# Four engines of a graph-network kernel take their instructions in source order from layer 1 on

## The chip, the cores and the metric

The kernel runs on one core of one Trainium2 chip. The metric is the device time in microseconds (us) of a whole execution. Five engines matter: PE (TensorE, matrix products; its weight loads are counted apart as PEld), DVE (VectorE), ACT (ScalarE), POOL (GpSimd) and SP (SyncE, which here only issues DMA transfers). Each engine works through its own list of instructions, and an instruction may wait for a semaphore that another engine or a transfer raises.

## The reference

A graph of 3125 nodes and 103125 directed edges (50000 random ones, the same turned round, and a self loop for each node), 128 features per node. Four residual layers follow one another, each inside a layer norm:

```
x = layernorm(x + relu(segment_sum(edge_weight * (x @ W)[src], dst) + b))      # layer 0
x = layernorm(x + gat(x))                                                      # layer 1
x = layernorm(x + attention(x))                                                # layer 2
x = layernorm(x + sigmoid(sage(relu(sage(x)))))                                # layer 3
```

`gat` has 4 heads of 32 features: `e = leaky_relu(a_src[src] + a_dst[dst], 0.2)`, a softmax of `e` over the edges that end in a node, the weighted sum of `(x @ W)[src]`, a bias, a linear skip path and an inner layer norm with gain and bias. `attention` has one head: the softmax over a node's incoming edges of query times key, then the weighted sum of values. A `sage` layer is the mean of the neighbours' features through one matrix plus the node's own through another.

## The kernel before

Nodes are padded to 25 blocks of 128 (`NB`), and every layer is made dense. A first stage turns the edge list into two matrices, through one-hot products on PE: `ctd`, the number of edges between any two nodes (bf16, 25 × 128 × 3200), and `wd`, the sum of their weights, both kept in DRAM. This stage and most of layer 0 share a loop: PE adds `wd` blocks times `x @ W` into five PSUM banks `acc0` (20 blocks of destination nodes; line 794). It ends at line 902 with `front.close()`.

**Layer 1.** What is left of layer 0 (destination blocks 20 to 24, banks `left`, weights loaded as `cw`) is added in a loop over 25 source blocks, and between its steps stand the first tasks of layer 1, by the number of the step (`marks`): `scores1` (transposes of x and the products with the attention vectors; line 1093 copies a part out to `ad`, which goes through the DRAM buffer `add_`), `heads`, `factors` (four exponentials), and from step 13 on four calls of `values(b)`, two blocks each. `values` (lines 1130 to 1144) scales x @ W by two exponentials on DVE and splits the result into three bf16 parts with `split3` (lines 549 to 555): ACT copies, DVE subtracts, ACT copies, DVE subtracts, ACT copies.

Then come 200 items: 4 groups of destination blocks (4, 7, 7, 7 blocks; `IG`), two head pairs each, 25 source blocks each. An item has masks and products. `masks` makes for each of two heads the edge mask for that side of the leaky relu: either an activation `fm` on ACT (line 1225) and a minimum `cm` on DVE (line 1226), or one DVE instruction (line 1219). `products` are three matmuls for each destination block (lines 1236 and 1241). The source writes `masks` two items ahead of `products`; there are 8 `cm` buffers, 5 `fm` and 6 `ct` (the counts from DRAM). In group 0's first head pair nine more calls of `values` stand in every second item. After the last item of a head pair `sums` reduces PSUM into `nz` on DVE (line 1260) and finishes on POOL (lines 1266 to 1269); `quotients` follows, and after the second head pair `finish1`: norm1 (statistics on DVE, a square root on ACT), norm2 (identities on ACT), three POOL operations, a second norm, and the transposes `turns` for layer 2 (line 984 and the lines near it). `skips` (lines 1249 and 1250) adds the skip path. These tasks are spread over items by a list of due steps:

```
def later(k, f):
    due.append((now[0] + k, f))
```

`step()`, called once per item, writes out the tasks that are due, so the source already has them at certain items.

**Layer 2** has 50 items: scores on PE (line 1373), exponential on ACT (1376), product with the counts on DVE (1377), one item ahead of the products with the values (1381). The tasks of `finish1` for the last group of layer 1 stretch into its first items, and `degrees` (line 1356) stands in its fourth. **Layer 3** multiplies with the counts twice (`add1`, line 1476; `add2`, line 1549) with the hidden layer between (`hidden`, lines 1505 to 1507, `around` and `own`, line 1513, which share one PSUM bank `tr`). The end (lines 1565 to 1577) takes seven groups of up to 4 blocks, one after the other in the source: a scaled sum on DVE, a sigmoid on ACT, the residual sum, a layer norm (statistics on DVE, square root on ACT line 767, up to four identities on ACT line 773) and the store.

**What sets the order.** Every engine's list is put in order when the kernel is built, by a scheduler that sees all instructions with their dependences and weaves tasks that don't depend on each other. Once built, the order is fixed. The square root, the exponential and the sigmoid use different function tables on ACT; the compiler puts a table load ahead of an activation whose table isn't in place.

Of the kernel before, what the change touches and what calls it, by code (L numbers as in the profile page):

```python
# [505 lines left out]
def fast_path(  # L506
# [403 lines left out]
        copy(xT[:, b0 * P : (b0 + n) * P], t[:, : n * P])  # L910


    lp = ctx.enter_context(tc.tile_pool(name="f_p12", bufs=1))
    xT = lp.tile([P, NP], F32, name="f_xT")

# [664 lines left out]
@with_exitstack  # L1580
def gnn_kernel(ctx, tc, *args):

    nc = tc.nc
    fl = ctx.enter_context(tc.tile_pool(name="fl", bufs=1))
    flag = fl.tile([1, 1], I32, name="flag")
    fast_path(tc, flag, *args)
    ok = nc.values_load(flag[0:1, 0:1], min_val=0, max_val=1, skip_runtime_bounds_check_because="a comparison's result")
    with tc.If(ok == 0):
        general_path(tc, *args)
# [30 lines left out]
```

## Time and profile before

| | us |
|---|---|
| median of 3 runs | 1537.32 (1535.15 to 1537.59) |
| profiled execution | 1536.56 |
| its span, first to last instruction | 1534.5 |
| PE busy | 1400.5 (91%) |
| DVE busy | 981.0 (64%) |
| ACT busy | 923.4 (60%) |
| POOL busy | 122.5 (8%) |

The span is 2.1 us shorter than the execution's time, which has the start and the end around it. The mean granted TensorE clock was 0.979. In a list of waits or groups, `fm<-adr,bas` is an output and what it is made from, by the program's names, and "<-DVE cm" names what ended a wait. In a timeline each row has its start, its length, the engine, the line, and how many instructions were put together in the row. All line numbers in the text are those of the kernel before; in the changed kernel they are larger by 4 from line 913 on.

### The profile page before, as it was taken

Reading aid. Unit: us, or ns where it says so; the run is one execution under the profiler, and the core shown is the slowest. Engines: PE = TensorE matmul, PEld = TensorE weight load, DVE = VectorE, ACT = ScalarE, POOL = GpSimd, SP = SyncE. Lnnn points to the kernel's source line nnn. Section 1 sums busy time; section 2 is a strip of 40 time slices with the busy share of each in tenths; the row PEclk is TensorE's granted clock in tenths of the full one; section 3 lists DMA queues with packets and bytes.
Section 4 is the critical chain, followed back from the end, with each engine's and each line's share of the span. In section 5 each row is a group of like instructions: output and inputs, shape, how many; then the busy total and the mean of one; then the engine's idle time right before and its main releaser. Section 6 shows DMA issues by size and latency. Waiting matters only on the chain.

```text
span 1534.5 us, 35155 instructions
## 1 busy us (share of the span) xinstructions
PE 1400.5 (91%) x14871; PEld 1223.6 (80%) x14871; DVE 981.0 (64%) x1574; ACT 923.4 (60%) x1880; POOL 122.5 (8%) x136
## 2 busy tenths in 40 slices
PE   4899999999997978899989989899999989999995
PEld 3898999998997867899979889577777764458995
DVE  4999899989991389778878887544464360012005
ACT  2988778888882489878778676544474340023006
POOL 1000000000000023203311320300000000000000
PEclk9999999999999999999999999999999999999998
DMA  6387787878877623444434333332222226513551
GB/s 192 91 220 207 203 234 206 235 202 223 214 214 232 222 85 101 143 118 125 132 115 134 114 87 95 106 94 68 67 72 73 82 105 238 193 44 129 195 195 45
DMA packets 210368, 224.39 MB, mean 146 GB/s; under 512 B 72892, under 2 KB 184007, under 8 KB 209945
## 3 DMA queue, kind: packets, MB, share of 16 engines
q1 hardware_dynamic: 206344, 217.74, 48.4%
q10 hardware_dynamic: 3457, 2.35, 0.6%
q8 instruction: 118, 1.93, 0.5%
q0 software_dynamic: 400, 1.97, 0.4%
q14 instruction: 49, 0.40, 0.1%
HBM read 157.67 MB, written 64.36 MB: 145 GB/s over the span
## 4 chain that ended last, share of the span: by engine, by line
PE 40%; DVE 5%; ACT 2%; issue 1%; POOL 1%; DMA 1%; DVEq 0%; ACTq 0%; SPq 0%; POOLq 0%
PE acc L1381 9%; PE s L1373 8%; PE acc L1476 7%; PE acc L1549 6%; PE acc L1241 4%; PE acc L1236 2%; DVE cm L1226 1%; DVE nz L1260 1%; PE tr L1513 1%; PE acc L1513 1%; DMA ct<-f_ctd 1%; ACT fm L1225 1%; DVE cm L1219 0%; PE tr L1505 0%; PE acc L1505 0%
## 5 line engine op out<-in xcount | busy, mean ns | idle before, releaser
L1241 PE MATMUL acc<-vp,cm 128*128 128x198 bf16 x2500 | 344.7, 252 | 6.6 <-DVE cm L1226 4.1
L1225 ACT ACTIVATE fm<-adr,bas 128x896 bf16<-128x896 f32 (+1 forms) x320 | 286.5, 952 | 68.0 <-DVE cm L1226 63.1
L1236 PE MATMUL acc<-vp,ct 128*128 128x204 bf16 x1250 | 315.2, 256 | 10.0 <-DVE vp L1144 5.6
L1241 PEld LDWEIGHTS <-cm 128*128 128x128 bf16 x2500 | 236.0, 98 | 26.5 <-issue 10.6
L872 PE MATMUL wp<-wod,ohc 128*128 128x128 bf16 x3840 | 244.0, 219 | 8.8 <-ACT cs L877 6.6
L872 PEld LDWEIGHTS <-ohc 128*128 128x128 bf16 x3840 | 224.0, 98 | 9.8 <-issue 9.4
L833 DVE TENSOR_TENSOR wod<-ohd,w 128x4096 bf16<-128x4096 bf16 (+1 forms) x120 | 225.0, 1931 | 0.6 <-PE wp L872 0.6
L1226 DVE TENSOR_TENSOR cm<-fm,ct 128x896 bf16<-128x896 bf16 (+1 forms) x320 | 198.1, 649 | 36.1 <-PE acc L1241 14.1
L842 ACT ACTIVATE wod<-ohd,wu 128x128 bf16<-128x128 bf16 x640 | 197.0, 400 | 0.0
L1377 DVE TENSOR_TENSOR e<-e,ct 128x416 f32<-128x416 f32 (+1 forms) x175 | 110.4, 636 | 108.2 <-ACT e L1376 102.6
L1376 ACT ACTIVATE e<-s,f_nm 128x416 f32<-128x416 f32 (+1 forms) x175 | 111.5, 642 | 99.4 <-PE s L1373 94.1
L1381 PEld LDWEIGHTS acc<-self__8127,e 128*128 128x128 f32 x1250 | 148.4, 193 | 21.5 <-issue 19.7
L1373 PE MATMUL s<-yT,f_xT 128*128 128x416 f32 (+1 forms) x350 | 145.8, 552 | 4.6 <-ACT rt L1356 4.0
L1381 PE MATMUL acc<-self__8127,e 128*128 128x129 f32 x1250 | 148.7, 276 | 0.6 <-DVE e L1377 0.6
L794 PE MATMUL acc<-f_xw,cw 128*128 128x128 f32 x1000 | 118.4, 278 | 7.4 <-DMA cw<-wd 7.4
L1236 PEld LDWEIGHTS <-ct 128*128 128x128 bf16 x1250 | 122.4, 98 | 2.5 <-issue 1.5
L883 ACT COPY ws<-wp 128x512 f32<-128x512 f32 x160 | 93.6, 585 | 49.8 <-PE wp L872 48.2
L794 PEld LDWEIGHTS acc<-f_xw,cw 128*128 128x128 f32 x1000 | 115.0, 194 | 7.6 <-DMA cw<-wd 7.6
L864 PE MATMUL cp<-ohc,ohd 128*128 128x125 bf16 x1280 | 96.7, 218 | 21.1 <-ACT ws L883 17.9
L1373 PEld LDWEIGHTS s<-yT,f_xT 128*128 128x128 f32 x350 | 62.2, 191 | 57.7 <-issue 40.6
L1476 PE MATMUL acc<-ct,ip 128*128 128x512 bf16 (+1 forms) x525 | 104.9, 360 | 1.4 <-DMA ct<-f_ctd 1.4
L1549 PE MATMUL acc<-ip,ct 128*128 128x128 bf16 x1875 | 105.2, 219 | 0.0
(277 smaller groups left out, 1482.7 us busy)
## 6 DMA issues: line engine op xcount, KB each, us to landing
ct<-f_ctd SPq DMA_DIRECT2D x50, 800.0 KB
wd<-ws SPq DMA_DIRECT2D x40, 896.0 KB
ct<-f_ctd SPq DMA_DIRECT2D x150, 224.0 KB
cw<-wd SPq DMA_DIRECT2D x50, 640.0 KB
f_ctd<-cs SPq DMA_DIRECT2D x20, 1000.0 KB
ct<-f_ctd SPq DMA_DIRECT2D x25, 416.0 KB
ct<-f_ctd SPq DMA_DIRECT2D x25, 384.0 KB
cw<-wd SPq DMA_DIRECT2D x25, 320.0 KB
```

The lines of the kernel that those rows point to most:

```text
L794: nc.tensor.matmul(accs[j // 4][:, j % 4, :], cw[:, j - h, :], xw[:, i, :], start=False, stop=(i == NB - 1 and (j % 4 == 3 or j == n - 1)) ...
L833: nc.vector.tensor_tensor(f[:, 0:n].rearrange("p w (a t) -> p w a t", t=2), ohd[:, 0:n].rearrange("p w (a t) -> p w a t", t=2), twos(w2[s] ...
L842: nc.scalar.activation(wod[2][:, BW + w, :], ohd[:, BW + w, :], AF.Copy, scale=w3[:, 1, at : at + 1])
L872: nc.tensor.matmul(wp[:, j, :], ohc[:, w, :], wod[s][:, w, :], start=(j == 0 and q == 0 and s == 0), stop=(j == 3 and q == 1 and s == 2), ...
L1225: nc.scalar.activation(f[:, : n * P], at, AF.Relu, bias=bas[:, c, h : h + 1], scale=UP)
L1226: nc.vector.tensor_tensor(m[:, : n * P], f[:, : n * P], ct[:, : n * P], OP.min)
L1236: nc.tensor.matmul(out_(F1, PW), ct[:, k * P : (k + 1) * P], vp[:, c, hp : hp + 2, :, 2 * F1 : V1], start=(c == 0), stop=False, skip_group ...
L1241: nc.tensor.matmul(out_(0, 2 * F1)[:, j], ms[j][:, k * P : (k + 1) * P], vp[:, c, hp + j, :, 0 : 2 * F1], start=False, stop=(c == NB - 1 a ...
L1373: nc.tensor.matmul(s[:, :m], xT[:, c * P : (c + 1) * P], yT[:, i0 * P + a : i0 * P + a + m], start=True, stop=True)
L1381: nc.tensor.matmul(acc[k // 3][:, (k % 3) * (P + 1) : (k % 3 + 1) * (P + 1)], es[q, c][:, k * P : (k + 1) * P], vo[:, c, 0 : P + 1], start ...
L1476: nc.tensor.matmul(acc[k][:, :n], ips[b // 4][:, b % 4, s, :], ct[:, c : c + n], start=(b == 0 and s == 0), stop=(b == NB - 1 and s == 2),)
L1549: nc.tensor.matmul(acc[g][:, j, :], ct[:, (b0 + j) * P : (b0 + j + 1) * P], ups[b // 4][:, b % 4, s, :], start=(b == 0 and s == 0 and j == ...
```

## The change

Between the end of layer 0's shared loop (and the small function `turned`) and the buffers of layer 1, a context is entered that stays open to the end of the kernel. Inside it the instructions of PE, DVE, ACT and POOL are issued in the order in which the source writes them. SP, which issues the transfers, is not in the list and is still placed by the scheduler. No instruction of the source is added, removed or altered; ACT's table loads are placed anew by the compiler, for the new order.

```diff
@@ -910,6 +910,10 @@
         copy(xT[:, b0 * P : (b0 + n) * P], t[:, : n * P])
 
 
+
+    ctx.enter_context(
+        tc.manual_schedule(engines={mybir.EngineType.PE, mybir.EngineType.DVE, mybir.EngineType.Activation, mybir.EngineType.Pool})
+    )
     lp = ctx.enter_context(tc.tile_pool(name="f_p12", bufs=1))
     xT = lp.tile([P, NP], F32, name="f_xT")
 
```

## The prediction

> **What bounds the kernel now.** I read the page's span, busy shares and 40 slices first, then the chain that ended last, the groups with what they waited for, and then one stretch at a time: busy time by window, TensorE's waits by window, and the timeline where an order had to be seen. The page first (a slice is 38.4 us):
>
> ```profile
> PE 1400.5 (91%) x14871; PEld 1223.6 (80%) x14871; DVE 981.0 (64%) x1574; ACT 923.4 (60%) x1880; POOL 122.5 (8%) x136
> PE   4899999999997978899989989899999989999995
> DVE  4999899989991389778878887544464360012005
> ACT  2988778888882489878778676544474340023006
> PE 40%; DVE 5%; ACT 2%; issue 1%; POOL 1%; DMA 1%; DVEq 0%; ACTq 0%; SPq 0%; POOLq 0%
> ```
>
> TensorE is the bound nearly everywhere: it is idle only 1534.5 − 1400.5 = 134 us, so an order can win at most that. It can lose more. The change touches nothing before about 437 us (layer 0's shared loop), so I look after that. Layer 1 runs from about 547 to 958 us, layer 2 to about 1250, layer 3 to the end. Busy time by window (window, length, then PE, PEld, DVE, ACT, POOL, granted clock, DMA share, GB/s):
>
> ```profile
> 547.70:598.80 51.10, 39.60 (x351) 33.73 (x352) 47.78 (x141) 48.44 (x90) 13.44 (x25) 0.93 0.29 86
> 629.20:958.00 328.80, 301.52 (x3215) 290.54 (x3215) 269.27 (x491) 248.51 (x324) 75.46 (x54) 0.98 0.40 117
> 958.00:1000.00 42.00, 36.18 (x196) 25.58 (x194) 21.43 (x69) 24.87 (x46) 12.39 (x10) 0.96 0.34 113
> 1000.00:1250.00 250.00, 250.00 (x1438) 184.55 (x1437) 115.35 (x235) 120.67 (x205) 1.68 (x1) 1.00 0.23 71
> 1505.00:1534.50 29.50, 11.07 (x199) 10.90 (x196) 16.02 (x83) 20.53 (x43) 0.00 (x0) 0.77 0.20 58
> ```
>
> Three kinds of stretch. In the first head pair of group 0 (547.7 to 598.8) DVE and ACT are the bound, 47.8 and 48.4 busy of 51.1: no slack. In groups 1 to 3 and layer 2, PE is, with slack on the others. In the last 29.5 us there is no PE bound but a chain through ACT and DVE.
>
> **What the Trainium skill says.** "PSUM — Partial Sum Buffer", section "Engine vs sequencer instructions": the queues of ScalarE, VectorE and GpSimdE are strict FIFO and matmuls start and complete in program order. So a compiled order is what runs, and an instruction that waits holds all behind it. The trace agrees: no instruction of DVE or ACT overtakes there. "ScalarE: Activation LUTs", section "What ACT_TABLE_LOAD costs": about 1283 ns for the load and about 1380 ns for a drain at each switch. The trace shows the 1.28 us, but no drain after other work: a sigmoid starts at 1507.22 and takes 0.61, the load begins at 1507.86, and the square root starts at 1509.15. I take 1.28.
>
> **The change part by part.** Nothing is added or removed; instructions of PE, DVE, ACT and POOL go in source order instead of an order that the scheduler wove, and the compiler then places ACT's table loads anew. In SP's queue a few stores and loads of `add_`/`adr` shift by a few places; it waits for nothing new that the before order does not already have (its 6 `ct` buffers run ahead).
>
> *A, the rest of layer 0 (437 to 547.7): 0.* The `left` accumulation is fed by `cw` loads at 231 GB/s (437 to 500) and ends with them. The four `values` chains placed among it are hidden under that; from −3 (nothing woven in) to +3 (a chain of 5 us outlasts it).
>
> *B, group 0, heads 0 and 1: +30.* One `values` (L1130–1144) is a ping-pong: DVE scales, ACT copies (L549), DVE subtracts, ACT, DVE, ACT, DVE negates (L1144):
>
> ```profile
> 536.15 0.75 DVE L1134 TENSOR_TENSOR v<-trw,fa 128x256 f32<-128x256 f32 x2
> 536.99 0.63 ACT L549 CAST vp<-v 128x528 bf16<-128x528 f32 x1
> 537.65 0.71 DVE L551 TENSOR_TENSOR vs<-v,vp 128x528 f32<-128x528 f32 x1
> 538.39 0.63 ACT L552 CAST vp<-vs 128x528 bf16<-128x528 f32 x1 [0.77 <-DVE vs L551]
> 539.06 0.71 DVE L554 TENSOR_TENSOR vs<-vs,vp 128x528 f32<-128x528 f32 x1 [0.70 <-ACT vp L552]
> 539.80 0.63 ACT L555 CAST vp<-vs 128x528 bf16<-128x528 f32 x1 [0.78 <-DVE vs L554]
> 540.47 0.64 DVE L1144 TENSOR_SCALAR vp<-vp 128x396 bf16<-128x396 bf16 x2 [0.37 <-ACT vp L555]
> ```
>
> It takes 541.11 − 536.15 = 4.96 us, with DVE working 2.81 and waiting 2.15. At 560 to 600 the scheduler fills these gaps with masks (DVE 38.9 busy of 40). In source order no mask stands between the links on either queue; 9 chains lie here, one every second item: 9 × 2.15 = 19.4. The two `scores1` blocks put an `ad` copy (L1093), which waits for PE, ahead of the masks' activations: about 3 + 2. `factors` has four exponentials with a table load each way: 1.4 not covered. The start: the masks of the first items stand behind the ends of both `left` blocks and the fourth chain, which end near 554, where the before order began masks at 547: +4. Sum 29.8. Bounds: 20 (chains alone) and 40. The later items of PE are behind it, so nothing covers it. The second head pair (598.8 to 629.2) is cover neither way: −1 to +2, I take 0.
>
> *C, groups 1 to 3: +3.* PE works 301.5 of 328.8, so up to 27 us are to be gained. Its longest waits there:
>
> ```profile
> PE few L1249 <- DVE f_xw L1250: 9.7, 5, 3.4
> PE few L984 <- ACT f_x L975: 5.8, 2, 2.9
> ```
>
> These are `skips` and `turns`, which the source spaces one or two items apart (1.85 us each), 9.7 and 5.8 and 4.0 more behind L990, so about 20 us of them should go. Against that, in source order a norm is a block: norm1 is 2.2 us on DVE, the square root needs a table load of 1.28, norm2's seven identities hold ACT 2.8 us ahead of the next mask. Masks are two items ahead, 3.7 us, so about 8 us reach PE where these meet, twice or less in a group, and 3 after each last item for `nz`: I take 30 against 27. Bounds: −15 (the distances of `later` cover nearly all) and +15.
>
> *D, start of layer 2 (958 to 1000): +2.* PE is idle 5.8 now, 4.0 of it at the degrees' transpose. `finish1` of group 3 stretches over layer 2's first items: POOL's three operations of 2.1 us, two norms, table changes between square root and exponential. About 8 against 6. Bounds −3 and +8.
>
> *E, layer 2 (1000 to 1250): 0.* PE is at 250.0 of 250, the others below half. The order can hardly touch it; to +2.
>
> *F, layer 3 up to 1498: +3.* Eight transposes that were moved up go back among the `add1` matmuls (8 × 0.1 = 0.8, an estimate from half a weight load of 0.19, since no row shows them apart), less 0.3 for a quicker drain at 1250; around 1392 to 1412 `own` and `around` share one `tr` bank and wait for a split chain each: 2.5. From 0 to +5.
>
> *G, the end: +13.* Each of seven groups goes sigmoid, add, statistics, square root, identities. Before, two groups share table loads; sigmoids after a load start at 1505.15, 1513.34 and 1521.15, so 7.8 for two groups:
>
> ```profile
> 1519.86 1.28 ACT L1568 ACT_TABLE_LOAD   x1
> 1521.15 0.63 ACT L1568 ACTIVATE t<-t 128x512 f32<-128x512 f32 x1
> 1521.69 1.63 ACT L773 ACTIVATE f_x<-f_xw,ms,sd 128x128 f32<-128x128 f32 x4
> 1523.23 0.29 ACT L1568 ACTIVATE t<-t 128x128 f32<-128x128 f32 x1
> ...
> 1524.02 1.28 ACT L767 ACT_TABLE_LOAD   x1 [0.50 <-DVE sd L766]
> ```
>
> In source order ACT has load, sigmoid, load, square root, four identities for each group, 14 loads in place of 8. The first sigmoid to the last identity of a group: 2.85 to the square root (1521.15 to about 1524.0; its load lies under DVE's 2 us), 0.65 to the first identity (1517.45 to 1518.10), 1.64 identities, then 1.28 for the sigmoid's load: 6.4 to 6.6 with hand-overs. From 1499.7: six periods of 6.5 end at 1538.7, the last group of one block takes 2.5: 1541.2, against 1528.0: +13.2. PE's 3.3 us per group hide under it. From +11 to +15.
>
> Sum: 0 + 30 + 0 + 3 + 2 + 0 + 3 + 13 = 51 on the profiled execution (1534.5 span, 1536.6 with what lies around it, 0.8 below the median of 1537.3). So 1536.6 + 51 = 1588; on the median 1588 too.
>
> **The rivals.**
> *Source order wins in C and D (0.22).* Speaks for it: the source already places `later` steps at distances, masks two items ahead, and PE's waits of 20 us have an owner. C −15, D −3, and B nearer 22: 22 − 15 − 3 + 2 + 13 = +19, 1556; up to about 1565.
> *It is faster (0.06).* The place is group 0: if the DVE gaps in the chains are covered (ACT far enough ahead that DVE loses only the start, 5) and C and D give all but a little of their 33 us, −28: 5 − 28 + 13 + 1 = −9, 1528. It decides where C and D's gain exceeds B plus 13. Against: in B the chains' links follow one another on both queues, which leaves at least 19, so C and D would have to yield everything.
> *Lockstep (0.10).* If ACT's identities and DVE's statistics stall PE at every norm (two norms and a boundary in each of three groups, 8 us each, say 48 above my C) the time is 1588 + 35 or so, 1620; a lower granted clock (0.77 where PE is idle at the end, 0.93 in B) would add to it.
> *Nothing changes (0.02).* Were the two orders alike it would be within 0.2%, about 3 us, which is what a measurement of this kernel can tell. Against: from the first `left` matmuls on, the compiled orders of PE, DVE, ACT and POOL differ everywhere.
>
> **How the numbers follow.** The forecast has 0.60, and 1570 to 1605 as its own range. With the second rival down to 1552 and a part of the lockstep case up to 1613, eight in ten are held. Faster by over 0.2% 0.06, within 0.2% 0.02, slower by over 0.2% 0.92.
>
> **What would show it.** B: chains without a mask between, DVE and ACT at 75 to 85% between 555 and 630, the first `nz` (L1260) near 629 instead of 598.8. C: skips' and turns' waits gone from PE, waits on `cm` L1226 in their place, PE's busy time unchanged. D: PE idle about 8. G: 14 table loads, sigmoids 6.5 apart. I would be wrong if group 0 ends before 615, or if groups 1 to 3 take over 345 or under 314 us against 328.8.

## The result and the profile after

The changed kernel takes 1623.34 us (median of 4 runs, 1623.30 to 1624.44) against 1536.99 for the kernel before in the same comparison: a ratio of 1.0566, 95% interval 1.0547 to 1.0584. It is 86 us slower; 51 were forecast, and the time lies above the stated range (1570 to 1605, with 1613 as the upper end of its wider one).

The page of the changed kernel, span, busy times, slices and chain (a slice is now 40.5 us):

```profile
span 1621.2 us, 35041 instructions
PE 1418.7 (88%) x14858; PEld 1233.6 (76%) x14871; DVE 1006.6 (62%) x1574; ACT 933.6 (58%) x1886; POOL 115.1 (7%) x136
PE   4999999899987766889979889989999989999990
DVE  4999998999933456878879878544455350021013
ACT  3988878887852456878678668444555330032025
PE 41%; DVE 11%; ACT 9%; issue 2%; DMA 0%; ACTq 0%; DVEq 0%
```

The work is the same. What grew is for the most part idle time: PE is idle 202.5 us instead of 134.0, and busy 18 us longer over the same matmuls. In the chain that ended last the share of DVE and ACT grew (5% and 2% before, 11% and 9% now). The hole in all three rows in slices 14 to 16 is the end of the `left` stretch and the first head pair of layer 1's group 0; there TensorE's granted clock fell too (0.76, against 0.93 before). Busy time by window, the stretches that answer to those of before:

```profile
500.00:554.30 54.30, 46.39 (x338) 40.30 (x339) 19.31 (x77) 19.87 (x44) 3.73 (x13) 0.94 0.53 172
554.30:645.00 90.70, 54.54 (x358) 44.37 (x357) 54.75 (x143) 52.53 (x92) 9.06 (x30) 0.76 0.17 48
677.00:1019.00 342.00, 305.37 (x3215) 290.21 (x3215) 280.90 (x492) 247.49 (x324) 73.65 (x54) 0.98 0.39 112
1019.00:1065.00 46.00, 37.66 (x204) 26.32 (x202) 28.38 (x69) 24.33 (x41) 12.78 (x10) 0.94 0.35 111
1065.00:1315.00 250.00, 249.87 (x1435) 184.68 (x1435) 114.11 (x232) 121.79 (x208) 1.68 (x1) 1.00 0.24 69
1570.00:1621.00 51.00, 14.29 (x256) 14.11 (x253) 19.41 (x95) 30.67 (x50) 0.00 (x0) 0.68 0.12 34
```

In 554 to 645 (547.7 to 598.8 before) DVE and ACT, the bound of that stretch, are busy 54.8 and 52.5 of 90.7, 60% and 58%, where they had been full. Landmarks of the two traces put the 86.7 us of the span in place:

| landmark | before | after | later by | added in the part |
|---|---|---|---|---|
| last `left` matmul starts (A) | 545.3 | 554.3 | 9.0 | 9.0 (forecast 0) |
| first `nz` of group 0, first head pair (B) | 598.8 | 645.1 | 46.4 | 37.4 (30) |
| `nz` of group 0, second head pair | 629.2 | 677.0 | 47.8 | 1.4 (0) |
| last `nz` block of group 3 begins (C) | 958.05 | 1019.05 | 61.0 | 13.2 (3) |
| last scores of layer 2 (D, E) | 1249.2 | 1313.7 | 64.5 | 3.5 (2) |
| last `add2` matmuls (F) | 1515.9 | 1584.1 | 68.2 | 3.7 (3) |
| end of the span (G) | 1534.5 | 1621.2 | 86.7 | 18.5 (13) |

### The profile page after: what moved, and what is told of

Read it like the earlier page. It is cut to its first block, busy times and chain, and to the rows that moved or that the text cites. A ratio compares the mean times of both kernels' runs of the same rounds, so it can differ in the third digit from the quotient of the medians.

```text
span 1621.2 us, 35041 instructions
## 1 busy us (share of the span) xinstructions
PE 1418.7 (88%) x14858; PEld 1233.6 (76%) x14871; DVE 1006.6 (62%) x1574; ACT 933.6 (58%) x1886; POOL 115.1 (7%) x136
## 4 chain that ended last, share of the span: by engine, by line
PE 41%; DVE 11%; ACT 9%; issue 2%; DMA 0%; ACTq 0%; DVEq 0%
PE s L1377 7%; PE acc L1385 7%; PE acc L1245 7%; PE acc L1480 6%; PE acc L1553 5%; PE acc L1240 4%; ACT fm L1229 3%; DVE cm L1230 3%; DVE nz L1264 1%; DVE cm L1223 1%; DVE e L1381 1%; ACT f_x L979 1%; DVE bs L965 1%; PE acc L1517 1%; ACT f_xw L979 1%
## 5 line engine op out<-in xcount | busy, mean ns | idle before, releaser
L1245 PE MATMUL acc<-vp,cm 128*128 128x198 bf16 x2500 | 360.5, 257 | 44.1 <-DVE cm L1230 29.5
L1240 PE MATMUL acc<-vp,ct 128*128 128x204 bf16 x1250 | 325.5, 260 | 8.7 <-DVE nz L1264 5.3
L1229 ACT ACTIVATE fm<-adr,bas 128x896 bf16<-128x896 f32 (+1 forms) x320 | 282.6, 950 | 31.7 <-DVE cm L1230 31.4
L1245 PEld LDWEIGHTS <-cm 128*128 128x128 bf16 x2500 | 241.7, 100 | 69.1 <-DVE cm L1230 37.0
L1230 DVE TENSOR_TENSOR cm<-fm,ct 128x896 bf16<-128x896 bf16 (+1 forms) x320 | 207.0, 674 | 58.6 <-ACT fm L1229 49.9
L1381 DVE TENSOR_TENSOR e<-e,ct 128x416 f32<-128x416 f32 (+1 forms) x175 | 114.5, 665 | 119.1 <-ACT e L1380 113.1
L1385 PEld LDWEIGHTS acc<-self__8129,e 128*128 128x128 f32 x1250 | 148.4, 193 | 19.7 <-issue 18.6
```

Of the source, the lines that this page charges most:

```text
L1229: nc.scalar.activation(f[:, : n * P], at, AF.Relu, bias=bas[:, c, h : h + 1], scale=UP)
L1230: nc.vector.tensor_tensor(m[:, : n * P], f[:, : n * P], ct[:, : n * P], OP.min)
L1240: nc.tensor.matmul(out_(F1, PW), ct[:, k * P : (k + 1) * P], vp[:, c, hp : hp + 2, :, 2 * F1 : V1], start=(c == 0), stop=False, skip_group ...
L1245: nc.tensor.matmul(out_(0, 2 * F1)[:, j], ms[j][:, k * P : (k + 1) * P], vp[:, c, hp + j, :, 0 : 2 * F1], start=False, stop=(c == NB - 1 a ...
L1385: nc.tensor.matmul(acc[k // 3][:, (k % 3) * (P + 1) : (k % 3 + 1) * (P + 1)], es[q, c][:, k * P : (k + 1) * P], vo[:, c, 0 : P + 1], start ...
```

## The experiments

All times are medians; what a run gained is against the changed kernel's 1623.3. Most runs have two executions, and the kernel before had medians from 1534.9 to 1537.8 in the comparisons, so a difference of 1 or 2 us says little by itself. In code, lines without a sign show the place, `...` marks a cut, `{...}` stands for the engines, and comments are added here. A line with an L is one of the run whose view is shown.

**Where the loss sits.** `e1_from_layer2`, the context entered only after layer 1:

```diff
-    ctx.enter_context(tc.manual_schedule(engines={...}))   # ahead of layer 1's buffers
+    ctx.enter_context(tc.manual_schedule(engines={...}))
     p3 = ctx.enter_context(tc.tile_pool(name="f_p3", bufs=1))
```

> Source order from layer 2 on only; layer 1 is woven by the scheduler as before. The trace of the changed kernel puts about 4 us of the loss at the start of layer 2, 6 at the middle of layer 3 and 19 at the end: 1537 + 29 = 1566. By the prediction's terms (D 2, F 3, G 13) it would be 1555. If the losses of layer 1 were only passed on to later stages by a lower clock or by late transfers, it is below 1550.

Measured: 1564.1 (ratio 1.0183, 1.0151 to 1.0214), 29 above the kernel before in the same comparison (1534.9), 27 above its 1537.0. The three parts of the table for layers 2 and 3 have 25.7 together, and 26.9 in this run's trace: these layers lose by themselves about what the changed kernel's trace shows for them, so hardly anything is passed on from layer 1.

`e2_from_items`, the context entered ahead of layer 1's items, so that the `left` stretch is woven:

```diff
+        ctx.enter_context(tc.manual_schedule(engines={...}))
         items = [(g, hp, c) for g in range(len(IG)) for hp in range(0, H, 2) for c in range(NB)]
```

> Source order from the items of layer 1 on; the rest of layer 0, with the scores and the first four calls of values, is woven as before. If the order of PE in the left stretch is what makes group 0 start 10 us late, 1623 - 10 = 1613, and the last left matmul starts near 545. If the stretch is bound by its loads, as the prediction has it, and the late start comes from the items' own order, 1620 to 1623.

Measured: 1609.5, 14 less. The last `left` matmul starts at 545.6 and the first `nz` at 630.0, 31.2 later than before. So B, alone, costs what was forecast for it (30), and the order in the `left` stretch costs 15: 9 in the stretch and 6 in the start of the items. The starts of the chains (their first subtraction, L551) show where: from the last `left` matmul to the fifth chain it takes 13.5 us before, 17.3 in this run and 23.9 in the changed kernel; from there to the last chain 35.5, 59.3 and 59.2; from that to `nz` 4.5, 7.8 and 7.8. The 6 us lie ahead of the fifth chain.

`e3_not_the_end`, the context (here called `source`) closed ahead of the last stretch:

```diff
         last = {b: counts(b) for b in range(NB - HB, NB)}
+        source.close()
         for g, (b0, n) in enumerate(GB):
```

> Source order up to the last stretch; the seven groups of the end are woven as before. By the trace of the changed kernel the end costs 19: 1604. By the prediction's term 13: 1610.

Measured: 1604.7, 18.6 less: the end costs what the trace shows.

**The left stretch.** TensorE's waits from 500 to 560 us in the changed kernel (engine and line, what it waited for, total, times, longest):

```profile
PE tr_sa L1091 <- ACT f_xT L532: 3.6, 3, 2.2
PE left L794 <- DMA cw<-wd: 3.1, 1, 3.1
PE acc L1240 <- DMA ct<-f_ctd: 2.2, 1, 2.2
PE tr_sa L1091 <- DVE f_xT L534: 1.6, 2, 0.8
```

`scores1` has a transpose, a copy on another engine, and products that need the copy. In source order PE stands through each copy, and through the first load, with `left` matmuls behind; the scheduler had put these in between. `e7_scores_two_steps` writes the products one or two steps of the loop after the transposes:

```diff
-        marks = {3: lambda: scores1(0), 4: lambda: (scores1(1), scores1(2)), 5: lambda: scores1(3), 6: lambda: scores1(4)}
+        marks = {
+            2: lambda: turn1(0), 3: lambda: (turn1(1), score1(0)), 4: lambda: (turn1(2), score1(1)),
+            5: lambda: score1(2), 6: lambda: turn1(3), 7: lambda: score1(3), 8: lambda: turn1(4), 9: lambda: score1(4),
+        }
...
-        marks[7] = top
-        marks[9] = ...
+        marks[10] = top
+        marks[11] = ...
```

> The changed kernel, with each scores1 of the left stretch written in two steps: transposes and copy at one step of the loop, the products that need the copy at a later one. Theory: the left stretch ends 9 us late because PE, busy 46 of 48 us there before, waits in order for each copy and for the first load; about 5 of it are waits for copies: 1618, last left matmul near 550. Rival: the loads bind the stretch, as the prediction has it: 1623.

Measured: 1621.8, 1.6 less, which by itself is hardly more than the comparisons differ. The stretch itself, first to last `left` matmul, took 47.9 us instead of 51.5 (41.4 before), so this edit gave back 3.6 of the 10; a wait of 1.8 for a copy and the 3.1 for the load are still there. The first `nz` came 3.8 earlier (641.4), but by the last `nz` of group 3 only 1.7 were left. The theory holds in part for the stretch, and half of the gain is used up in later waits.

`e8_pe_woven` takes PE out of the list:

```diff
-        tc.manual_schedule(engines={mybir.EngineType.PE, mybir.EngineType.DVE, ...})
+        tc.manual_schedule(engines={mybir.EngineType.DVE, ...})
```

> The changed kernel without PE in the list: DVE, ACT and POOL in source order, PE woven. If the losses come from the order of DVE and ACT (chains, norms, table loads), only the left stretch's 9 us come back: 1614. If PE's order is the cause of the late start as a whole (15 us in the run whose source order began with the items), 1608. If weaving PE alone hurts, because the scheduler's guess of DVE and ACT is off, over 1623.

Measured: 1609.3, 14 less. The last `left` matmul starts at 545.2, as before: the 9 us of A are PE's order. The first `nz` comes at 639.5, only 5.7 earlier, so B's own chains stay, and of the 9 us 3.4 are used up there. The time is near the 1608 of the second theory, but not for its reason: the late start did not come back as a whole, and the rest of the 14 lies in groups 1 to 3 (3.6) and in layers 2 and 3. From the last `add1` to the first `add2` it takes 12.2 us as before (1449.5 to 1461.7), against 18.2 in the changed kernel: F's loss is PE's order too. The end, from first sigmoid to last, is 43.7 us as in the changed kernel: that is ACT's and DVE's order.

**The chains of group 0.** One period of the changed kernel (timeline: start, length, engine, line; rows of PE and POOL left out):

```profile
577.50 0.63 ACT L549 CAST vp<-v 128x528 bf16<-128x528 f32 x1 [1.28 <-DVE v L1138]
...
578.16 0.71 DVE L551 TENSOR_TENSOR vs<-v,vp 128x528 f32<-128x528 f32 x1 [0.75 <-ACT vp L549]
578.91 0.63 ACT L552 CAST vp<-vs 128x528 bf16<-128x528 f32 x1 [0.78 <-DVE vs L551]
579.57 0.71 DVE L554 TENSOR_TENSOR vs<-vs,vp 128x528 f32<-128x528 f32 x1 [0.70 <-ACT vp L552]
580.31 0.63 ACT L555 CAST vp<-vs 128x528 bf16<-128x528 f32 x1 [0.78 <-DVE vs L554]
580.85 1.33 ACT L1229 ACTIVATE fm<-adr,bas 128x512 bf16<-128x512 f32 x2
580.98 0.45 DVE L1148 TENSOR_SCALAR vp<-vp 128x396 bf16<-128x396 bf16 x2 [0.70 <-ACT vp L555]
```

DVE waits 0.75, 0.70 and 0.70 in each chain, 2.15 as forecast, and no mask stands between. From chain to chain it takes 9.9 and 9.0 us at first, with the second block of `scores1` and `factors` in between, and then 6.5 to 7.2. `e5_values_woven` writes the links apart, one mask between two, and each mask's activation one mask ahead:

```diff
-                values(ready)
+                chain = values(ready, False)      # first link; the other three are returned
...
-                masks(*items[y_])
+                if items[y_][0] == 0:
+                    for j_ in range(2):
+                        if x_ % 2 and chain:
+                            chain.pop(0)()
+                        half()                     # fm of the next mask, then cm of this one
+                        if x_ % 2 == 0 and j_ == 0 and chain:
+                            chain.pop(0)()
+                else:
+                    masks(*items[y_])
```

> The changed kernel, with the links of each chain of values in layer 1's first head pair written apart, one mask between two links, and each mask's activation written one mask ahead of its minimum. Theory: nine chains lose 2.15 us each because no mask stands between their links; woven by hand the period of two items falls from about 6.7 to 5.3: 9 x 1.4 = 12 less, 1611, and the first reduction after the first head pair (nz) starts near 633 instead of 645. Rival: DVE and ACT are short of work there for another reason (PE behind its copies, or counts that land late): the period stays and it is 1620 to 1625.

Measured: 1609.5, 13.8 less; the first `nz` at 631.3 instead of 645.1. From chain to chain it now takes 5.3 us, as the theory had it, and from the fifth chain to the last 46.7 instead of 59.2. So this part of the loss is the unwoven order of chains and masks, and a source order that weaves gets it back. The edit does two things, links apart and activations ahead; which gave how much wasn't tested. It is also little more than a third of B: 24 of its 37 us stay.

`e15_masks_first` puts the first three items' masks ahead of the ends of the `left` blocks:

```diff
+        for y_ in range(3):
+            masks(*items[y_])
         for g, (b0, n) in enumerate(left):
             end0(acc1[g], b0, n)
```

> The changed kernel, with the masks of layer 1's first three items written ahead of the ends of both left blocks. Source order from the items on gave back 15 us at the first reduction (nz), of which the left stretch explains 9. Theory: the other 6 are the ends of the left blocks (5.4 us of DVE from 559.7 to 564.8) that stand ahead of the first masks: nz near 640 instead of 645, 1618. Rival: the first products are then only earlier in waiting for the next item, since the ends must be done for scores1 anyway: 1622 or more.

Measured: 1626.0 (1622.9 and 1629.1), not faster. The trace is of the slower of the two executions. In it the first mask came 5.4 us after the last `left` matmul instead of 10.5, yet `nz` came 89.8 after it instead of 90.8: the gain is 1 us and not 5, as the rival has it. That this execution is slower comes for the larger part from the stretch ahead, 55.5 us against 51.5. Busy time by window of this run, its first half, against the changed kernel's: PE at a granted clock of 0.67 and 0.87.

```profile
504.20:530.00 25.80, 22.13 (x105) 16.76 (x106) 6.20 (x34) 8.70 (x21) 0.00 (x0) 0.67 0.52 182
```

```profile
502.80:528.60 25.80, 21.33 (x124) 16.35 (x125) 6.87 (x34) 9.22 (x22) 0.00 (x0) 0.87 0.56 195
```

With PE busy as long, 105 matmuls were done there and not 124. What gave the lower clock in one run wasn't tested.

**Groups 1 to 3.** TensorE's waits from 677 to 1019 us in the changed kernel:

```profile
PE acc L1245 <- DVE cm L1230: 15.5, 10, 3.9
PE few L992 <- DVE f_xT L534: 5.8, 3, 2.9
PE acc L1240 <- DVE nz L1264: 4.4, 3, 2.7
PE few L992 <- ACT f_xT L532: 2.7, 2, 2.1
PE few L988 <- ACT f_x L979: 2.6, 3, 1.1
PE few L1253 <- DVE f_xw L1254: 2.6, 4, 1.0
```

The masks' row before, from 629 to 958 us:

```profile
PE acc L1241 <- DVE cm L1226: 2.6, 5, 0.8
```

PE is idle 36.6 us against 27.3. The `skips` (L1253) did give back 7 of their 9.7. The turns did not: their second step now waits 8.5 for a copy (L992), and with 2.6 behind an identity that makes 11 against 10 before. The copy of the longest wait, at 831.3, stands in DVE's queue behind two masks, which wait for ACT. New are 13 more for masks. The rest of the 13.2, 3.9, is PE being busy longer over the same matmuls (305.4 against 301.5). ACT's timeline, group 2:

```profile
804.57 0.21 ACT L970 ACTIVATE sd<-sd 128x7 f32<-128x7 f32 x1 [7.08 <-DVE sd L969]
804.68 1.96 ACT L1229 ACTIVATE fm<-adr,bas 128x896 bf16<-128x896 f32 x2
807.70 2.80 ACT L979 ACTIVATE f_xw<-f_xw,ms,sd 128x128 f32<-128x128 f32 x7 [1.07 <-DVE ms L977]
810.41 6.62 ACT L1229 ACTIVATE fm<-adr,bas 128x896 bf16<-128x896 f32 x7
```

The square root stands in ACT's queue and waits for the statistics, 7.08 us idle, with the mask activations behind it. `e6_root_later` writes it one item later, in both norms of layer 1, with what follows:

```diff
-        nc.scalar.activation(sd, sd, AF.Sqrt)
+        later(1, lambda: nc.scalar.activation(sd, sd, AF.Sqrt))
...
-            later(gap[0], first_scale)
+            later(1 + gap[0], first_scale)
```

> The changed kernel, with the square roots of layer 1's inner and outer norm written one item later and all that follows them too. In the changed kernel the root stands ahead of an item's mask activations on ACT and waits for DVE's statistics (ACT idle 7.1 us at 797.6 to 804.6), and groups 2 and 3 take 6 us more each in their first head pair. Theory: that wait is the cause of about half of it: 1623 - 6 = 1617, with ACT's wait gone. Rival: the 2.8 us of identities and POOL's claim on DVE's speed are the cause: 1622 to 1626, since the chain is one item longer.

Measured: 1614.5, 8.8 less, but not where it was expected. Groups 2 and 3 gave 2.6 in their first head pairs, and group 1 as much, of which the second head pairs took back 2.0; ACT's wait was 4.8 still. The larger part came at the start of layer 2: from the last `nz` of group 3 to the last scores it took 288.3 us instead of 294.7. There PE had waited 7.4 us, 6.7 of it once, for an exponential that stood behind a root and its table load; now the total is 0.7:

```profile
PE s L1377 <- ACT e L1380: 7.4, 3, 6.7
```

```profile
1058.82 1.28 ACT L970 ACT_TABLE_LOAD   x1 [7.55 <-DVE sd L969]
...
1061.63 1.60 ACT L1380 ACTIVATE e<-s,f_nm 128x416 f32<-128x416 f32 x3
```

```profile
PE s L1380 <- ACT e L1383: 0.7, 3, 0.3
```

(The first two are the changed kernel, waits from 1020 to 1066 us and ACT's timeline, the third is this run from 1015 to 1060, with its lines 3 larger.)

`e12_identities_halved` writes norm2's seven identities in two halves, one item apart:

```diff
-            norm2(keep["a"], r, r, i0, n)
+            norm2(keep["a"], r, r, i0, n, 0, n // 2)
+            later(1, first_rest)
```

> The changed kernel, with norm2's identities of layer 1's inner and outer norm written in two halves, one item apart. Theory: seven identities (2.8 us on ACT) ahead of the next mask activation are the second cause in groups 2 and 3: 1623 - 4 = 1619. Rival: the longer chain of the norm gives it back, or POOL's three operations alone starve PE: 1623 to 1626.

Measured: 1622.2 (1620.8 to 1623.7): no difference that this run can tell. The turns wait less (2.9 for copies), the masks as long or longer.

`e9_masks_three_ahead`:

```diff
-            for y_ in range(x_ if x_ == 0 else x_ + 2, min(x_ + 3, len(items))):
+            for y_ in range(x_ if x_ == 0 else x_ + 3, min(x_ + 4, len(items))):
```

> The changed kernel, with layer 1's masks written three items ahead of their products instead of two (the buffers allow it). Theory: in groups 2 and 3 DVE's minima run at 1.8 us and more instead of 0.6 while POOL's three operations run, and ACT's identities stand ahead of the mask activations, so the stock of masks gives out (PE waits 15.5 us for cm in groups 1 to 3); one item more, 1.85 us a time and some eight times, takes 8 to 12 off: 1613. Rival: the stock can't be filled because ACT and DVE have no time to spare there: 1621 to 1624.

Measured: 1638.0, 15 slower, a case that neither theory had. From 640 us to the end of layer 1 PE waits less for masks, 11.0 us instead of 17.0, but 16.3 instead of 5.3 for `nz` at the boundaries between head pairs, and 9.3 instead of 2.6 for the identities ahead of the turns. The largest single loss is the second head pair of group 0, 36.8 us instead of 31.8. DVE's timeline of this run ahead of that boundary:

```profile
673.41 0.75 DVE L1223 SCALAR_TENSOR_TENSOR cm<-adr,nas,ct 128x512 bf16<-128x512 f32 x1 [1.67 <-DMA ct<-f_ctd]
...
680.20 0.63 DVE L1230 TENSOR_TENSOR cm<-fm,ct 128x896 bf16<-128x896 bf16 x1 [3.04 <-DMA ct<-f_ctd]
...
681.80 2.02 DVE L1264 TENSOR_REDUCE nz<-acc 128x134 f32<-128x402 f32 x4
```

A mask further ahead needs buffers for itself and for its counts, and by the source these come free with the products, which the last items of a head pair delay. That is read from the source and these waits, not tested apart. In source order the mask that waits stands ahead of `nz` in DVE's queue.

`e13_no_pool_three` and `e14_before_no_pool_three` leave out POOL's gain, bias and residual of the inner norm, in the changed kernel and in the one before:

```diff
-            nc.gpsimd.tensor_tensor(rs, rs, g_row[:, None, :].to_broadcast([P, n, P]), OP.mult)
-            nc.gpsimd.tensor_tensor(rs, rs, b_row[:, None, :].to_broadcast([P, n, P]), OP.add)
-            nc.gpsimd.tensor_tensor(rs, rs, xs, OP.add)
```

> The changed kernel without POOL's three operations of each group's inner norm (gain, bias and residual are left out, so what follows sees other numbers). Theory: what is left of the 6 us that groups 2 and 3 each lose is POOL's hold on DVE, during which the minima take 1.8 us instead of 0.6 with only two items of masks in stock: 10 less over the groups and the start of layer 2, 1613, where the kernel before would lose only 2 or 3 by the same edit because its scheduler has placed other work there. Rival: POOL's operations cost both orders the same; then the edit takes as much off both.

> The kernel before with the same three operations left out of each group's inner norm. Theory: 1534 or so, 2 to 3 less than 1537. Rival: as much less as in source order, some 10: 1527.

Measured: 1612.1 in source order, 11 less; 1515.7 before, 22 less (ratio 0.9859, 0.9830 to 0.9888). Neither the theory nor the rival held (the 11 in source order is near the theory's 10, but its reason falls with the second run): the order before pays more for these three operations, 5 us in the first head pair of each of groups 1 to 3 (61.5 to 56.7 in group 2) and 5.6 after the last `nz`. Source order gets 0.8, 1.8 and 3.2 there, and 6.4 after: with POOL out of the way its other waits in the groups are still there. So these operations of POOL are not what makes source order slower: without them the two orders lie further apart, 96 us and not 86. Of the 12 us in groups 2 and 3 the roots explain 2.6; the rest is a sum of waits for masks, copies and turns that no single edit took away, and stays open.

**The end.** ACT's timeline, a period with the load under DVE's work and one without:

```profile
1574.29 0.63 ACT L1572 ACTIVATE t<-t 128x512 f32<-128x512 f32 x1
1574.93 1.28 ACT L767 ACT_TABLE_LOAD   x1
1577.07 0.21 ACT L767 ACTIVATE sd<-sd 128x4 f32<-128x4 f32 x1 [0.85 <-DVE sd L766]
...
1580.67 0.63 ACT L1572 ACTIVATE t<-t 128x512 f32<-128x512 f32 x1
1583.49 1.28 ACT L767 ACT_TABLE_LOAD   x1 [2.19 <-DVE sd L766]
1584.79 0.21 ACT L767 ACTIVATE sd<-sd 128x4 f32<-128x4 f32 x1
```

In the first two groups the load for the square root starts as the sigmoid ends. From the third on it starts 2.2 us later, when DVE is done, and the root after it: a period of 7.72 us and not 6.39. The theory: from the third group on the root has two waits, for DVE and for its own engine (a buffer of a pool of two that comes round), and the compiler puts the first of them on the load. The trace shows the load's wait for DVE, but not how many waits a root has. `e4_seven_buffers`:

```diff
+        own3 = st.enter_context(tc.tile_pool(name="f_own3", bufs=7))
...
-            t = lp.tile([P, 4, P], F32, name="t3")[:, 0:n]
+            t = own3.tile([P, 4, P], F32, name="t3")[:, 0:n]
...
-            layer_norm(lp, x, r, (b0, n), True)
+            layer_norm(own3, x, r, (b0, n), True)
```

> The changed kernel, with seven buffers in place of two for the small tiles of the end (t3, bs, mv, sd, ms). In the changed kernel the table load for the square root waits for DVE from the third group on and the period is 7.72 us instead of 6.39. Theory: with two buffers the square root has a second wait, for a buffer, and the compiler puts the first one on the load; with seven buffers there is none and the load runs under DVE: period 6.39 throughout, 5 x 1.3 = 6.5 less, 1617. Rival: the period is the chain's own or the wait is put there for another reason: 1623.

Measured: 1615.7, 7.6 less. From the first sigmoid to the end of the span it is 46.8 us instead of 53.3, 6.5 less, and the period is 6.38 throughout, as in these rows of its ACT timeline, the fourth group's. That the number of buffers decides is shown; that it does so through a second wait is the theory, which fits.

```profile
1585.48 0.63 ACT L1573 ACTIVATE t<-t 128x512 f32<-128x512 f32 x1
1586.12 1.28 ACT L767 ACT_TABLE_LOAD   x1
1588.25 0.20 ACT L767 ACTIVATE sd<-sd 128x4 f32<-128x4 f32 x1 [0.84 <-DVE sd L766]
```

`e10_before_new_end` is the kernel before with an end in source order that shares table loads among groups 0 to 2 and 3 to 6 and normalises half of the blocks on DVE:

```diff
-            layer_norm(lp, x, r, (b0, n), True)
+        for g in range(3):
+            summed(g)
+            stats(g)
+        norms(0, 2)
...
+        norms(3, 6)
```

> The kernel before, with the end alone in source order and rewritten: groups 0 to 2 and 3 to 6 share their table loads (4 instead of 8), and half of the normalising goes from ACT to DVE. The last sigmoid should come 6 us earlier and the last row 6 us earlier than 1528: 1531, ratio 0.996. If the order before was already bound by PE's last group and the transfer out, 1536.

Measured: 1537.3 against 1537.1, ratio 1.000 (0.999 to 1.0009), no gain. Half the loads did not help: the sigmoids of groups 3 to 5 follow one another by 3.58 us, which is one group's own chain through both engines (sum 1.12, sigmoid 0.63, residual 0.69, statistics 0.87 and 0.36 with the hand-overs), and that began only when the first batch was normalised.

`e11_all_in_source` has the woven values, the two-step scores, the later roots, the new end, and in layer 3 `own` written ahead of `around`'s split:

```diff
-                around(k - 2)
+                t2 = second(ap.tile([P, 512], F32, name=f"acc3_{k - 2}"), k - 2, w2l)
             if 0 <= k - 3 < K:
                 own(k - 3)
+            if 0 <= k - 2 < K:
+                ups[k - 2] = in_parts(lp, k - 2, t2)
```

> The changed kernel with the repairs together: woven values (14 less by its own run), roots one item later (9), scores in two steps (2), own ahead of around's split in layer 3 (3), and the new end (19 + 6). If they add up: 1623 - 53 = 1570. If repairs in layer 1 share their gain (both give DVE and ACT time in the same stretch), 1575 to 1585.

Measured: 1579.3, 44 less, where 53 would be the sum. Layer 1 adds up: by the last `nz` of group 3 it is 19.6 earlier, where the woven values, the scores and the roots gave 13.9, 1.7 and 3.5 by themselves. What is missing is the end, 18 less and not 25, and `own`, 0.8 and not 3. The end, written by hand in source order, now takes what it took before, 18.9 us from the last `add2` against 18.6. The whole is still 42 slower than the order before; 28 of that are there by the first `nz` (626.7 against 598.8), and 12 come in groups 1 to 3. No version that computes the whole result beats the kernel before.

## Why the prediction was right or wrong

The direction and its main reason held; the size did not, 86 against 51. A and G, above all, came out beyond the bounds that the forecast gave them. Of its signs, a late `nz` (645, later than the 629 named), the 14 table loads and PE's idle time at the start of layer 2 (8.3 us, about 8 forecast) came true, and neither of the two that would have refuted it appeared (group 0 ended after 615, groups 1 to 3 took 342 us and not over 345). DVE and ACT at 75 to 85% in B did not: 59% and 55% from 555 to 630. Part by part:

**A, 0: wrong, 9.0.** The step that failed is "fed by `cw` loads at 231 GB/s (437 to 500) and ends with them". The rate is that of the stretch before; from 500 to 547.7 PE was busy 46.1 of 47.7, so PE was the bound there and a wait in its queue had no cover. In source order PE waits there for copies (5.2 us) and once for a load (3.1). With PE woven the last `left` matmul is as early as before; 5.7 of the 9 us are left of that at the first `nz`.

**B, 30: right in its mechanism and nearly in its size.** By itself it is 31.2 (source order from the items), and the terms fit too: from the fifth chain to the last 23.8 more (19.4 for the chains' waits and some 3 for the second scores and `factors` were forecast), and 3.8 ahead of the fifth (4 for the start, 3 for the first scores). 3.3 behind the last chain were not forecast. The 6 us beyond lie ahead of the fifth chain and come with the order of the `left` stretch; masks written ahead of its ends gave back only 1, and what they are in detail is not settled.

**C, 3: the wrong value of a range that held it, 13.2 (−15 to +15).** Failed: "so about 20 us of them should go". 7 went. I took a wait at a turn as a matter of distance in the source, but in source order the copy that it waits for stands behind masks on DVE or ACT, and the turns wait 11 us where they had waited 10. Waits for masks grew by 13. An item was put at 1.85 us, which holds for the second head pairs (46.6 for 25); over groups 1 to 3 it is 2.2 (328.8 for 150), so distance in time wasn't what lacked. How these waits divide among roots, identities and the rest stays open.

**D and E, 2: 3.5,** with one of the causes named, table changes between root and exponential: exponentials stood behind a root (6.7 in one wait).

**F, 3: 3.7,** 0.4 at the start and 3.3 in the middle, net. The wait that was named is there: 3.2 us of PE, from 1461 to 1480, for the bank `tr` (2.0 at line 1517 and 1.2 at 1509 of the changed kernel). But it is not all of it. From the last `add1` to the first `add2` it takes 6.0 us longer, and the `add2` matmuls then take 2.7 less (104.7 against 107.4); and with `own` ahead of the split 0.8 came back. So part of the near hit is luck.

**G, 13: mis-sized, 18.5.** The mechanism, two table loads for each group, is right, and so is 6.39 for the first two periods. The step that failed is "its load lies under DVE's 2 us": that is so in the first two groups, and with seven buffers in all of them, but with the kernel's two buffers five loads of 1.28 came out from under cover (6.5 us). Without that the term would have been 12.

The sum of the mis-sized terms, 9 (A), 7 (B), 10 (C) and 5.5 (G), and 4 in small ones, is the 35 us that were missing. The rival of lockstep has nearly the time that was measured, 1620, but not its mechanism: groups 1 to 3 took 10 us more than the forecast for them, not 48. The rival in which C and D win is excluded, and with it the faster one: of the gain that they had to draw on, only the 7 us of the skips came. The fallen clock of group 0 was named with the lockstep rival. Groups 1 to 3 (0.98) and layer 2 (1.00) had the clock that they had before; what it costs in group 0, where PE is not the bound, no run takes apart.

The forecast took its table load from the Trainium skill, "ScalarE: Activation LUTs", section "What ACT_TABLE_LOAD costs", and left out the drain of 1380 ns that the section adds. The trace of the changed kernel bears out both choices: the load takes 1.28 us as the section says, and the section's drain is not seen after a sigmoid, which starts at 1574.29, takes 0.63, and is followed by the load at 1574.93.

## What to carry to other kernels

A hand order has to weave what the scheduler wove, or it loses it. Before giving a scheduler up, find in the profile where the bound engines are full (here DVE and ACT at 97% and 98% from 560 to 600 us, PE at 97% in the `left` stretch ahead), and ask which chains between engines lie there, since each link of an unwoven chain leaves one engine idle. Read the bound of a stretch from that stretch's own window, not from the one ahead of it. And an instruction that waits for another engine is dear where other work stands behind it: layer 1's square roots one item later were worth 9 us, and masks one item earlier, ahead of `nz`, cost 15.

## What the runs showed of the hardware that was not expected

A table load can wait for the work that the activation behind it needs. From the third group of the end on the load waits for DVE, 2.2 us, and costs its 1.28 in full; in the first two groups, and with seven buffers in all, it ran under DVE's work. Seven buffers in place of two, no other change, took 6.5 us off the end. The same wait is seen at the start of layer 2, 7.55 us at 1058.82.

POOL's three operations cost the order before more than source order (22 and 11 us), although DVE's minima stretch in both while they run: from 0.62 to 1.5 us before (2 in 3.06, at 761.38) and to 1.8 after (4 in 7.12, at 811.47). Of the changed kernel's 240 minima of 128x896, none of the 189 that no instruction of POOL overlaps takes over 0.63 us; where POOL is at work for more than half of a minimum, it takes 1.37 in the median.
